# Routing of the first half at the end of a scan, last logits among the first expert tiles, and two projections of kept chunks per step, in a two-layer graph and expert kernel

## The chip, the cores and the metric

The kernel runs on one core of one Trainium2 chip. The metric is device time in microseconds (us) of one execution. The core has a matrix engine (PE, with its weight loads shown as PEld), a vector engine (DVE), an activation engine (ACT), a general engine (POOL), and a queue that issues transfers (SP). They run side by side and wait for one another by semaphores; each works through its own queue in order.

## The reference

Input are x, 4096 tokens of 256 features, and an adjacency matrix of 4096 x 4096. Two layers follow one another; each is a graph part and an expert part, both added to x:

```python
x = x + L0_gnn(layernorm(x), adj)      # relu(adj @ x @ gcn_w + b), layernorm, mamba
x = x + L0_ffn(layernorm(x))           # top 2 of 8 experts, D=256, H=512, gelu
x = x + L1_gnn(layernorm(x), adj)      # filtered adjacency, projections, relu
x = x + L1_ffn(layernorm(x))           # top 2 of 6 experts, three layers
```

The mamba of layer 0 is a recurrence over the tokens with 512 channels and 16 states each:

```python
def step(hst, inp):
    dAt, dBut, Ct = inp
    hst = dAt * hst + dBut
    return (hst, hst @ Ct)
...
y = ys + u * D_skip
y = y * jax.nn.silu(z)
return y @ w_out
```

The expert part of layer 0 takes softmax of `xf @ gate_w + gate_b`, keeps each token's two largest, and adds `weight * (gelu(xf @ w1 + b1) @ w2 + b2)` of both experts.

## The kernel before

**The scan.** The 4096 tokens are cut into eight chunks c = 0 to 7 of 512. A chunk has 32 steps i = 0 to 31; a step is one channel block m (four blocks of 128) and a pair of states. Per step ACT makes two tiles da (L1154), DVE runs the recurrence twice (L1161) and multiplies by C (hc, L1171), POOL makes db (L1138), and PE adds the products up in PSUM (L1188, `Step.total`). At the end of a block DVE multiplies by silu(z) (`Step.gate`, L1197). The region is written as a manual schedule: each engine executes in the order in which the loop over n = 32c + i issues.

**Tails.** The output projection of chunks 0 to 5 is put off: their gated outputs are kept in device memory (`keep_gated`). From chunk 6's step 8 on, `Tail.step` works through a list of tails, one entry per scan step: two entries with a product on PE (L929, and the residual by an identity matmul, L933), one `put` (ACT copies PSUM with a sum, L938; stores x1d, L943), and at the next step `squares` (L948, L952). The first three chunks have one idle entry more. Chunk 6's own tails are put into the list at chunk 7's step 5, behind the kept ones. `Norm` normalizes rows of chunks 0 to 6 during chunk 7 (L985), transposes them (L998) and makes router logits (L1010); `Last` does the projection of chunk 7, its first half at steps 22 and 25 and its second half (`add`, L1063) behind the scan's last gates. `Last.norm` makes the statistics of chunk 7 (L1077 to L1082), its normed rows (L1087), their store (L1091), the transposes (L1097), logits (L1104), and x1d's last rows (L1110, L1112).

**Routing of the first half.** `Dispatch.choose` (by `router`, L110 to L138) finds the two experts of tokens; `place` counts them by two matmuls (L231, L235) and a chain of twelve DVE operations (L240 to L266); `one_hot` writes four groups of one-hot rows (L273); `tables` (a generator, L311 to L424) makes the list of tiles by expert, compares slots (L359, L363, L364), multiplies with the one-hots on PE (L369), and from that makes `src`, the row numbers to gather (L381 to L387), the bias sums (L395, L400) and `dst`. They follow the scan in program order: choose, place, `last.norm`, one_hot, tables; the engines' queues then hold them in an order set by a scheduler.

**Expert tiles.** `expert_tiles` goes through tiles of 256 rows of one expert: gather by `src` (L430, POOL), weights and bias (L532, L535, SP), transposes (L539), a copy to xkT (L543), first product ps_h (L518) with gelu (L522), second product ps_y (L503) of the tile before, bias (L508), store (L439). The first nine tiles are of the first half's tokens (part0[0]), the others of all tokens. Between tiles `then0` takes pieces of `others()`: choose, place, one_hot for the second and third batch, and their tables. Layer 1's adjacency tiles (L1498, L1504, L1505, L1506) are worked on beside them, and layer 1's propagation (L1516) comes after.

Of the kernel before, what the change touches and what calls it, by code (L numbers as in the profile page):

```python
# [9 lines left out]
F32 = mybir.dt.float32  # L10
# [20 lines left out]
def kernel(ctx: ExitStack, tc: tile.TileContext, out: bass.AP, **a):  # L31
# [73 lines left out]
    def router(ps, bias_b, E, rev, renorm, oh, wv, pool):  # L105
# [4 lines left out]
        nc.vector.tensor_tensor(lg, ps, bias_b.unsqueeze(1).to_broadcast([P, T, E]), ALU.add)  # L110
# [8 lines left out]
        nc.scalar.activation(lg, lg, AF.Exp)  # L119
        nc.vector.tensor_reduce(col(1), lg, AX.X, ALU.add)  # L120
# [6 lines left out]
        for i in range(2):  # L127
# [6 lines left out]
            if i == 0:  # L134
                nc.vector.scalar_tensor_tensor(lg, hots[0], -4.0, p, ALU.mult, ALU.add)
                q = lg
        if not renorm:
# [25 lines left out]
    class Dispatch:  # L163
# [47 lines left out]
        def choose(self, b, logits, bias_b, renorm, pool):  # L211
            T, t0 = self.T[b], self.t0[b]
            hots = self.oh[b][:, 1:, :].rearrange("p (t i) e -> p t i e", i=2)
            router(
                logits, bias_b, self.E, self.rev[:, :T, :], renorm, hots,
                self.wv[:, t0:t0 + T, :], pool,
            )

        def place(self, b, psum, tag, pool):

# [6 lines left out]
            if (2 * G + 1) * E <= CW:  # L227
                tot = ps[:, G * E:]
            else:
                tot = psum.tile([P, CW], F32, name="ps_pl1", tag=tag)  # L230
# [6 lines left out]
            )  # L237
            flat = pool.tile([P, E * (G + 1)], F32, name=f"pl_at{G}")
# [15 lines left out]
            )  # L254
            row = pool.tile([P, G], F32, name=f"pl_row{G}")
# [13 lines left out]
        def one_hot(self, b):  # L269

            g0, G, S, row = 2 * self.t0[b], 2 * self.T[b], 2 * TPC, self.row.pop(b)
            for g in range(0, G, S):
# [3 lines left out]
                )  # L276

    class Part:
# [14 lines left out]
        def tables(self, ps, tp, biases, NG, other=None, hots=None):  # L293
# [4 lines left out]
            if hots is None:  # L298
                def hots(shape):
                    return tp.tile(list(shape), BF16, name="tb_eq", bufs=3)  # L300
# [27 lines left out]
            nc.vector.tensor_reduce(ex, ge[:, :, 1:], AX.X, ALU.add)  # L328
            oh = ge[:, :, :E]
# [23 lines left out]
            S = 2 * TPC  # L353
            group = dp.group.rearrange("p t i -> p (t i)")
            slots = slot.rearrange("p f h -> p (f h)").unsqueeze(1).to_broadcast([P, S, C])
            for g0 in range(0, NG, S):
# [11 lines left out]
                for g in range(S):  # L368
                    nc.tensor.matmul(  # L369
                        ps[:, :2 * C], dp.lo[:, g0 + g, :], eq[:, :2, g, :],  # L370
                        start=(g0 + g == 0), stop=(g0 + g == NG - 1),
                    )
# [15 lines left out]
            nc.vector.tensor_scalar(ex, ex, float(E - 1), None, ALU.min)  # L388
            nc.vector.tensor_copy(self.exps, ex)
# [104 lines left out]
    def expert_tiles(jobs, psum, pool, weights, bias_out, layers, kb_out, also=None):  # L494
# [16 lines left out]
        def layer(w, xT, mb, func, bias, name):  # L511
            hT = pool.tile([P, mb, TR], F32, name=name)
            for mm in range(mb // 2):
                ps = ps_h.tile([P, 2, TR], F32, name="ps_h")
                for j in range(2):
                    m = 2 * mm + j
                    for d in range(DB):
                        nc.tensor.matmul(  # L518
                            ps[:, j, :], w[:, d, m * P:(m + 1) * P], xT[:, d, :],
                            start=(d == 0), stop=(d == DB - 1),  # L520
                        )
# [1273 lines left out]
```

## Time and profile before

| what | value |
| --- | --- |
| three runs, device time | 2415.34, 2420.55 (median), 2423.94 us |
| profiled execution, device time | 2412.49 us |
| its span | 2410.7 us |
| PE busy in the span | 2239.3 us (93%) |
| DVE busy | 1648.1 us (68%) |
| ACT busy | 1194.8 us (50%) |
| POOL busy | 1144.8 us (47%) |
| scan's recurrence, L1161 | 512 instructions, 1266 ns each |
| hc, L1171 | 256 instructions, 1281 ns each |
| first product of the tiles, L518 | 864 matmuls, 388 ns each |
| gelu's line L522, first wait | 11.39 us idle before it, at 1288.88 us |

The span runs from the first to the last instruction of the profiled execution; the 1.8 us between it and the device time lie around it. A duration is that of one instruction, and matmuls overlap, so their durations are longer than the distance between two of them: a group of x8 that shows 1.89 us in sum is the length of the group. In lines of the timeline, the bracket tells how long the engine was idle before the group and which instruction released it. The windows give busy time of each engine between two times.

### The profile page before, as it was taken

What the parts mean: (1) busy time and instruction counts of PE and PEld (TensorE: products, weight loads), DVE (VectorE), ACT (ScalarE), POOL (GpSimd) and SP (SyncE); (2) the same over time, 40 slices, a digit from 0 to 9 for tenths busy, and PEclk for the clock granted to TensorE, in tenths of its full rate; (3) what the DMA queues carried; (4) which work ended last, traced back from release to release, by engine and by line L of the source; (5) the groups of instructions that cost most, each with busy time, mean ns of one, the idle gap of its engine ahead of it and who ended that gap; (6) DMA issues with size and microseconds to landing.
All of it is one profiled execution on the core that took longest, in us unless ns stands there. A gap on an engine that the chain in (4) does not pass through costs nothing. (4 is left out here: it accounts for less than half of the span.)

```text
span 2410.7 us, 28097 instructions
## 1 busy us (share of the span) xinstructions
PE 2239.3 (93%) x9018; PEld 1624.2 (67%) x9018; DVE 1648.1 (68%) x2455; ACT 1194.8 (50%) x2050; POOL 1144.8 (47%) x828
## 2 busy tenths in 40 slices
PE   8999999999999999896997999799999999999985
PEld 7665665656465665553666888667888888877774
DVE  2069999999999999998986411291666667742233
ACT  4255666574655666574753322145555555532321
POOL 1057777777877787775644555310000000045652
PEclk9999999999999999998997999999999999999998
DMA  7279999999999999996848877551444444456786
GB/s 237 83 228 227 241 275 238 274 243 268 247 260 258 238 274 238 271 269 174 270 136 266 295 231 228 162 166 53 143 146 148 146 145 146 148 170 209 230 274 235
DMA packets 293071, 511.58 MB, mean 212 GB/s; under 512 B 25376, under 2 KB 159648, under 8 KB 292016
## 3 DMA queue, kind: packets, MB, share of 16 engines
q1 hardware_dynamic: 246640, 412.64, 54.5%
q0 software_dynamic: 46272, 97.03, 18.7%
q8 instruction: 75, 1.23, 0.2%
q14 instruction: 84, 0.69, 0.1%
HBM read 406.03 MB, written 44.83 MB: 187 GB/s over the span
## 5 line engine op out<-in xcount | busy, mean ns | idle before, releaser
L1138 POOL TENSOR_TENSOR db<-du,bb 128x1024 f32<-128x1024 f32 x256 | 607.1, 2372 | 329.5 <-DVE hc L1171 83.1
L1161 DVE TENSOR_TENSOR_SCAN db<-da,state,db 128x512 f32<-128x512 f32 x512 | 627.2, 1266 | 31.5 <-ACT da L1154 29.3
L671 PE MATMUL pt<-at,gn 128*128 128x256 f32 x2048 | 479.4, 387 | 14.9 <-ACT gn L87 9.2
L671 PEld LDWEIGHTS pt<-at,gn 128*128 128x128 f32 x2048 | 397.1, 195 | 135.7 <-issue 63.1
L1154 ACT ACTIVATE da<-dt,negA 128x512 f32<-128x512 f32 x512 | 346.4, 688 | 249.5 <-DVE db L1161 238.7
L1516 PE MATMUL pf<-gn,f 128*128 128x256 f32 x2048 | 452.0, 380 | 0.0
L1516 PEld LDWEIGHTS pf<-gn,f 128*128 128x128 f32 x2048 | 386.6, 190 | 57.2 <-issue 6.4
L1171 DVE TENSOR_TENSOR hc<-db,cb 128x1024 f32<-128x1024 f32 x256 | 328.0, 1281 | 18.2 <-issue 0.4
L1188 PE MATMUL psy<-hc,ident 128*128 128x512 f32 x576 | 301.6, 618 | 4.6 <-DMA hc<-hc 3.7
L81 POOL TENSOR_TENSOR ln_rs<-ln_rs,mhalf 128x4 f32<-128x4 f32 (+1 forms) x25 | 33.4, 1335 | 507.6 <-DVE ln_rs L80 507.1
L508 DVE TENSOR_TENSOR yk<-ps_y,bk 128x512 f32<-128x512 f32 x73 | 50.4, 691 | 308.9 <-PE ps_y L503 232.2
L1505 ACT ACTIVATE f<-f 128x1024 f32<-128x1024 f32 x128 | 134.6, 1057 | 198.7 <-DVE f L1504 128.2
L518 PE MATMUL ps_h<-xkT,wk 128*128 128x256 f32 x864 | 213.6, 388 | 14.7 <-DVE xkT L543 6.9
L503 PE MATMUL ps_y<-wk,hk 128*128 128x256 f32 x864 | 213.3, 382 | 9.2 <-ACT hk L522 6.6
L1175 POOL DMA_DIRECT2D hc<-hc x224 | 195.0, 870 | 0.2
L518 PEld LDWEIGHTS ps_h<-xkT,wk 128*128 128x128 f32 x864 | 159.1, 192 | 50.6 <-ACT hk L522 11.3
L1504 DVE TENSOR_SCALAR f<-at 128x1024 f32<-128x1024 f32 x128 | 88.1, 688 | 148.0 <-PE pf L1516 134.4
L503 PEld LDWEIGHTS ps_y<-wk,hk 128*128 128x128 f32 x864 | 161.9, 191 | 32.7 <-ACT hk L522 8.4
L1188 PEld LDWEIGHTS psy<-hc,ident 128*128 128x128 f32 x576 | 109.3, 196 | 90.2 <-issue 64.0
L1511 DVE SCALAR_TENSOR_TENSOR cnt<-at,cnt 128x1024 bf16<-128x1024 f32 x120 | 145.9, 1216 | 15.9 <-DMA at<-in_adjT_dram 12.3
L1506 ACT ACTIVATE f<-f 128x1024 f32<-128x1024 f32 x128 | 134.5, 1055 | 3.4
L787 PE MATMUL ps_xz<-hT,w_in 128*128 128x512 f32 x256 | 116.3, 597 | 15.2 <-ACT hT L771 8.8
(321 smaller groups left out, 2513.6 us busy)
## 6 DMA issues: line engine op xcount, KB each, us to landing
at<-in_adjT_dram SPq DMA_DIRECT2D x256, 512.0 KB
bb<-bcd SPq DMA_DIRECT2D x128, 512.0 KB
cb<-bcd SPq DMA_DIRECT2D x128, 512.0 KB
hc<-hc POOLq DMA_DIRECT2D x224, 256.0 KB
wk<-in_L_ffn_W_dram SPq DMA_DIRECT2D x70, 512.0 KB
wk<-in_L_ffn_expert_w_dram SPq DMA_DIRECT2D x114, 256.0 KB
yg<-d_ys SPq DMA_DIRECT2D x14, 512.0 KB
yd<-us SPq DMA_DIRECT2D x6, 1024.0 KB
```

The costliest lines, as they stand in the source:

```text
L503: nc.tensor.matmul(ps[:, j, :], hT[:, m, j * P:(j + 1) * P], w[:, m, :], start=(m == 0), stop=(m == kb_out - 1),)
L518: nc.tensor.matmul(ps[:, j, :], w[:, d, m * P:(m + 1) * P], xT[:, d, :], start=(d == 0), stop=(d == DB - 1),)
L671: nc.tensor.matmul(pt[:, k, :], xl[:, j, k * P:(k + 1) * P], at[:, jj, :], start=(j == 0 and k == 0), stop=(j == NT - 1 and k == DB - 1),)
L1138: nc.gpsimd.tensor_tensor(self.db, self.f.du[self.half][:, self.mi:self.mi + 1, :].to_broadcast([P, 2, CW]), self.bb, ALU.mult,)
L1154: nc.scalar.activation(da, self.f.dt[self.half][:, self.mi, :], AF.Exp, scale=negA[:, self.m, n:n + 1])
L1161: nc.vector.tensor_tensor_scan(self.db[:, j, :], da, self.db[:, j, :], state[:, self.m, n:n + 1], ALU.mult, ALU.add,)
L1171: nc.vector.tensor_tensor(self.hc, self.db, self.cb, ALU.mult)
L1175: nc.gpsimd.dma_start(self.hc[:, 0, :], self.hc[:, 1, :], accum_op=ALU.add)
L1188: nc.tensor.matmul(f.psy[m], ident, self.hc[:, j, :], start=False, stop=(self.g == GS - 1 and j == last),)
L1505: nc.scalar.activation(f, f, AF.Square)
L1511: nc.vector.scalar_tensor_tensor(cnt, at, 0.0, cnt, ALU.is_gt, ALU.add)
L1516: nc.tensor.matmul(pf[:, t, :], f[:, jj, t * P:(t + 1) * P], gn[:, j, :], start=(j == 0 and t % 2 == 0), stop=(j == NT - 1 and t % 2 == 1),)
```

## The change

Five things are changed together.

1. `router`, `place` and `one_hot` become generators (`choosing`, `placing`, `one_hots`), and a new generator `first_half` strings them together with the tables. The scan's loop takes one step of it at chunk 7's steps 24, 26, 28 and 31 (the router in three parts, then the place's two matmuls), takes two more before the last gates (the place's DVE chain), and the others after the gates and after the last projection.
2. `tables` gets `held`: the products with the one-hots (`products`) are issued together when all comparisons are done, into a PSUM bank that is asked for only then. The number of experts of tiles (`exps`) is written earlier. Its scratch tiles, and the first two gathered tiles `ready`, lie in the unused half of `gn` (`Carve`), and the two gathers are issued before `last.norm`.
3. `Last.norm` loses transposes and logits. Its normed rows are loaded back from device memory, and `logits7` makes the logits between the second and third batch's routing. Its stores go out on ACT's queue in place of SP's.
4. The router of the second batch, the bias sums' consumer and the second tiles' transposes are given an explicit order (`behind`, `turned`, `begun`); `then0` takes four pieces per tile from the second tile on, where it took three from the first. The order of PSUM pools changes, and the bank tag of `Last.first` (d2 to d0).
5. `TAILS`: two steps of `Tail.step` per scan step from chunk 6's step 24 to 31, none at chunk 7's steps 0 to 3.

```diff
-    def router(ps, bias_b, E, rev, renorm, oh, wv, pool):
+    def router(ps, bias_b, E, rev, renorm, oh, wv, pool, behind=None):
...
-        nc.vector.tensor_tensor(lg, ps, bias_b.unsqueeze(1).to_broadcast([P, T, E]), ALU.add)
+        op = nc.vector.tensor_tensor(lg, ps, bias_b.unsqueeze(1).to_broadcast([P, T, E]), ALU.add)
+        if behind is not None:
+            after(op, behind)
...
         nc.scalar.activation(lg, lg, AF.Exp)
+        yield
...
+        def placing(self, b, psum, tag, pool, second=None):
...
+                psum, tag = second or (psum, tag)
                 tot = psum.tile([P, CW], F32, name="ps_pl1", tag=tag)
...
+            yield
             flat = pool.tile([P, E * (G + 1)], F32, name=f"pl_at{G}")
...
-        def tables(self, ps, tp, biases, NG, other=None, hots=None):
+        def tables(self, ps, tp, biases, NG, other=None, hots=None, held=False):
...
+            nc.vector.tensor_scalar(ex, ex, float(E - 1), None, ALU.min)
+            nc.vector.tensor_copy(self.exps, ex)
...
+                eqs[g0] = eq
+                if not held:
+                    products(ps, g0)
+                yield
+            if held:
+                ps = ps()
+                for g0 in range(0, NG, S):
+                    products(ps, g0)
                 yield
...
-            nc.vector.tensor_scalar(ex, ex, float(E - 1), None, ALU.min)
-            nc.vector.tensor_copy(self.exps, ex)
...
-            xk = pool.tile([P, 2, D], F32, name="xk", bufs=4)
-            dp.fetch(k, xk)
+            if ready:
+                xk = ready.pop(0)
+            else:
+                xk = pool.tile([P, 2, D], F32, name="xk", bufs=4)
+                dp.fetch(k, xk)
...
+                    if d == 0 and j == 0 and given and 2 <= len(turned) < 4:
+                        after(op, begun[len(turned) - 2])
...
+        TAILS = {(NC - 2, i): 2 for i in range(24, STEPS)}
+        TAILS.update({(NC - 1, i): 0 for i in range(4)})
...
-                    nc.sync.dma_start(tokens(dp.xd, c)[:, t0:t0 + 2, :], xn[:, :2, :])
-                    ps_t = (ps_m if hh == 0 else ps_a).tile(
-                        [P, DB, HW], F32, name="ps_xnT7", tag=("m0", "d0")[hh]
-                    )
...
+                    nc.scalar.dma_start(tokens(dp.xd, c)[:, t0:t0 + 2, :], xn[:, :2, :])
...
-                    nc.sync.dma_start(rows, self.xr[hh])
+                    nc.scalar.dma_start(rows, self.xr[hh])
+
+        def first_half(biases):
+
+            yield from dp.choosing(0, lgs[:, :dp.T[0], :], gate_b, False, ra)
+            yield
+            yield from dp.placing(0, ps_m, "m0", ra, (ps_m, "m1"))
+            yield
+            table = part0[0].tables(
+                lambda: ps_m.tile([P, CW], F32, name="ps_inv", tag="m0"),
+                room, biases, NT, held=True,
+            )
+            next(table)
+            for _ in dp.one_hots(0):
+                next(table)
+            yield
+            yield from table
...
-                Tail.step(tails)
+
+                for _ in range(TAILS.get((c, i), 1)):
+                    Tail.step(tails)
...
+                    if i in (24, 26, 28, STEPS - 1):
+                        next(firsts)
...
+            next(firsts)
+            next(firsts)
             for k in gated:
                 steps[k].gate()
+            next(firsts)
             for m in range(H, MB):
                 for hh in range(2):
                     last.add(hh, m)
-        dp.lo = onehots
-        dp.choose(0, lgs[:, :dp.T[0], :], gate_b, False, ra)
-        dp.place(0, ps_y, "psy", ra)
+            next(firsts)
+            next(firsts)
+            ready = [room.tile([P, 2, D], F32, name="xk", bufs=2) for _ in range(2)]
+            for k, xk in enumerate(ready):
+                part0[0].fetch(k, xk)
         last.norm()
...
+            def logits7(xn):
+                xT = rp.tile([P, 2, DB, HW], F32, name="xnT7", bufs=1)
+                for hh in range(2):
+                    ps = inverse().rearrange("p (k t) -> p k t", k=DB)
...
+                    nc.scalar.copy(xT[:, hh], ps)
+                    yield
...
+                nc.scalar.copy(lgs[:, NT - TPC:, :], ps)
+                yield
+
             def others():
 
+
+                xn = rp.tile([P, TPC, D], F32, name="xn7", bufs=1)
+                nc.sync.dma_start(xn, tokens(dp.xd, NC - 1))
                 for b in (1, 2):
+                    if b == 2:
+                        yield from logits7(xn)
                     t0 = dp.t0[b]
-                    dp.choose(b, lgs[:, t0:t0 + dp.T[b], :], gate_b, False, rp)
+                    dp.choose(b, lgs[:, t0:t0 + dp.T[b], :], gate_b, False, rp, turned[0])
...
-                if n < FIRST0 - 2:
-                    for _ in range(3):
+                if 0 < n < FIRST0 - 2:
+                    for _ in range(4):
                         next(pieces, None)
```

## The prediction

> **What bounds the kernel now.** Four views, in this order: the page's busy shares, the windows by stage, the timeline between the scan and the first tiles, and the timeline of a stall in the scan's last chunk.
>
> PE is busy 93% of the span, DVE 68%: PE is the bound on average, so what counts is where PE does not work. The windows say where. The columns are length, then busy time of PE, PEld, DVE, ACT, POOL, the granted clock, DMA share and GB/s:
>
> ```profile
> 1060.00:1080.00 20.00, 20.00 (x60) 10.15 (x59) 16.04 (x13) 16.86 (x35) 13.48 (x10) 1.00 1.02 286
> 1080.00:1100.00 20.00, 11.13 (x31) 6.32 (x29) 19.55 (x17) 14.44 (x28) 9.71 (x7) 0.84 0.86 221
> 1100.00:1120.00 20.00, 8.81 (x26) 5.80 (x26) 19.73 (x18) 9.40 (x27) 17.25 (x8) 0.76 0.65 171
> 1140.00:1160.00 20.00, 20.00 (x64) 11.79 (x63) 14.50 (x12) 16.18 (x38) 9.41 (x4) 1.00 0.60 193
> 1256.00:1286.70 30.70, 11.18 (x67) 7.46 (x66) 21.94 (x117) 9.88 (x19) 9.77 (x10) 0.58 0.60 196
> 1345.00:1500.00 155.00, 153.48 (x750) 132.00 (x749) 37.41 (x52) 43.98 (x88) 83.19 (x84) 1.00 0.80 251
> ```
>
> In the scan the bound is DVE (19.55 of 20), except at 1140 to 1160, where it has only 14.50 of work: it waits there. From 1080 to 1120 PE has 20 us of room. From 1256 to 1286.7 PE works 11.18 of 30.70 us at a clock of 0.58: this is the gap between the scan's end and the first expert tile. From there on the tiles are bound by PE (153.48 of 155).
>
> The gap, link by link (start, duration, engine, line, operation; idle before it in brackets):
>
> ```profile
> 1245.63 1.23 DVE L1171 TENSOR_TENSOR hc<-db,cb 128x1024 f32<-128x1024 f32 x1
> 1247.13 5.40 PE L1188 MATMUL psy<-hc,ident 128*128 128x512 f32 x12
> 1252.36 3.62 PE L1063 MATMUL ps_out<-w_out,us 128*128 128x256 f32 x16
> 1256.93 0.70 DVE L240 TENSOR_TENSOR_SCAN pl_at<-onesf,ps_pl 128x264 f32<-128x264 f32 x1 [0.48 <-PE ps_pl L235]
> 1262.36 4.62 DVE L273 TENSOR_TENSOR gn<-iota,pl_row 128x1024 bf16<-128x1024 f32 x4
> 1275.21 0.17 DVE L387 CAST d0f_src<-tb_tok 128x18 int32<-128x18 f32 x1
> 1276.34 1.18 POOL L430 DMA_INDIRECT xk<-d_xdf,d0f_src  x1 [15.75 <-DVE d_oh L133]
> 1283.01 0.48 PE L539 MATMUL ps_xt<-ident,xk 128*128 128x128 f32 x1 [5.98 <-DMA xk<-d_xdf,d0f_src]
> 1285.28 0.69 DVE L543 COPY xkT<-ps_xt 128x512 f32<-128x512 f32 x1 [5.78 <-issue]
> 1286.92 5.02 PE L518 MATMUL ps_h<-xkT,wk 128*128 128x256 f32 x12
> 1288.88 0.47 ACT L522 ACTIVATE hk<-ps_h,d0f_b 128x256 f32<-128x256 f32 x1 [11.39 <-issue]
> ```
>
> The last hc (scan's end), totals, last projection, then the place chain, one-hots, tables, src, the gather (6.67 us from issue to the transpose), xkT, first ps_h. DVE is the chain's carrier from 1256.9 to 1275.4.
>
> The stall in chunk 7:
>
> ```profile
> 1137.28 1.89 PE L929 MATMUL ps_out<-w_out,at 128*128 128x256 f32 x8
> 1139.64 0.39 ACT L938 ACTIVATE xr<-ps_out 128x256 f32<-128x256 f32 x1 [5.45 <-PE ps_out L933]
> 1141.16 2.46 DVE L1161 TENSOR_TENSOR_SCAN db<-da,state,db 128x512 f32<-128x512 f32 x2 [7.83 <-ACT da L1154]
> 1148.07 1.28 ACT L811 ACT_TABLE_LOAD   x1
> ```
>
> A kept product (1.89 us and 0.59 for the residual, 2.48) stands late on PE; ACT's put waits for it, da stands behind the put, and the scan waits 7.83 us for da.
>
> [...]ps_h x8 takes 3.62 us from 1286.92 and 1.89 in full tiles; but the clock also halved around 1232, behind 1.19 us of full idleness among thin matmuls. [...]here the load is 1.28 and the next activation starts 1.30 after it, so I take 1.28. [...]the table operations agree, 0.15 to 0.22 us whether 8 or 72 elements. [...]the gather here takes 6.67, and that is used.
>
> **The change, part by part.** The sum is made on the profiled execution: 2412.5 us (span 2410.7), 8.1 below the median 2420.55 of the three runs.
>
> 1. Places at the scan's end. The router's twenty operations of the first half already stand among the last scan steps (the last at 1245.45), so they move little. The place's two matmuls (0.61 + 0.64, now at 1255.8) go ahead of the last two totals: PE would do one total (1.8), the two matmuls, then the other totals, so they end at about 1250.2 (1248.4 if ahead of all three). The place's twelve DVE operations add up to 3.87 us (0.70, 0.15, 0.41, 0.14, 0.41, 0.61, 0.59 and five of 0.17); they run from 1250.2 to 1254.1. Both gates (0.69 each, now 1250.84 and 1252.56) are queued behind them on DVE: 1254.1 and 1254.8. The last projection waits for the gates and ends about 2.5 us later than 1256.0; from 1.25 (PE alone) to 3.6 (if PE's clock halves while it waits). Behind it stand the norm of chunk 7 and its stores.
>
> 2. Tables behind the gates. From 1254.8: tables some 20 operations at 0.16 = 3.3, chunk 7's statistics between them 2.0, one-hots 4.62 and the pairs at L359/L364 8 x 0.3 = 2.4 with 1.3 for ACT's L363 between: 8.3. That is 1268.4; products 0.4, the seven operations to src 1.6 (1273.68 to 1275.38 now, whose way held an f at L1504): src at about 1270.4, against 1275.38. **5.0 us earlier**; 4.4 to 7 by the bounds of part 1 and of the interleaving.
>
> 3. From src to PE at work. The gather follows 5.0 earlier, xkT is there at about 1280.9, and ps_h could start at 1282. But the bias sums, the router of the second batch and f are moved behind xkT, and ACT has Exp (0.27), L1505 and L1506 (1.06 each) and a table load (1.28) ahead of the first gelu. From 1280.9: three router operations to 1281.6, f (0.69) by 1283.0, the two of ACT to 1285.1, the load to 1286.4. The first gelu is then 2.5 us earlier than 1288.88, not 5.0. PE has five groups to do until it needs it, so part of the rest survives: I take **-3.0**, bounds -5.0 and 0. The lower end of the gain is the weights: on SP's queue the reload of chunk 7's normed rows, which waits for the last stores, is put ahead of at, b1 and wk (now 1270.85), so wk goes out at 1272 to 1274, and when wk landed is not shown.
>
> 4. Last logits among the tiles. Eight transposes (1.04 in the trace for such eight) and sixteen matmuls (1.85) leave a stage where PE idles and enter one where PE is the bound: **+2.9**. An Exp of the second batch among gelus needs two table loads, 2.56 us on ACT, which is busy 43.98 of 155 there; ps_h's three buffers hide most: **+0.4** (0 to 1.5).
>
> 5. Tails. Two steps per scan step from chunk 6's i24, none in chunk 7's i0 to i3; the kept ones end at i19 of chunk 7, not i23. In chunk 7 the put no longer stands ahead of da at 1139.6: ACT goes from zs (1134.2) over the squares (1.6) to da, and the scan resumes near 1136 instead of 1141.2. The next put still waits for a product behind the second zs group (PE at about 1147.7), with a table load behind it, so scan steps that now start at 1153.4 and 1157.4 start at about 1150.5 and 1154.2: **-3.2** (-5 to 0). PE freed at i20 to i23 (4 x 2.48) lies beside a scan bound by DVE: **-0.6** (0 to -1.2, DVE's idle time at 1200 to 1220). In chunk 6 the added products find PE full until 1080 and put and squares (2.8 us per tail) find ACT at 16.86 of 20; after 1081 there is room: **+0.5** (0 to 9.9, four steps of 2.48 if all is handed to the scan).
>
> Sum: -3.0 + 2.9 + 0.4 - 3.2 - 0.6 + 0.5 = -3.0. On the profiled execution 2409.5, on the scale of the median **2417.5**.
>
> **Rivals.** No change means within 0.3%, 7.3 us, about what these runs tell apart (they spread over 8.6).
>
> - *Faster, 2410.5.* The 5.0 us of src come through whole because PE's five groups and a warmer clock cover gelu's wait, part of the logits' matmuls (2) fill holes in the first tile, and the stall at 1141 goes nearly whole: -5.0 + 0.9 + 0.4 - 5.0 - 1.2 = about -10. For it: PE's clock of 0.58 in the gap. Against: ACT's queue ahead of the first gelu.
> - *Slower, 2430.* The same stall in a new place: chunk 6, i24 to i31. Every second tail step is a put that waits on ACT for products on a full PE, with da behind it; four doubled steps are 9.9 us of backlog until PE has room, and DVE, busy 19.55 of 20 from 1080 on, can't make that up. With chunk 7's gain used up by the same lateness: -3.0 + 3.3 - 0.6 + 9.9 = +9.6. It decides from 7.6 us lost there. For it: PE 20.00 of 20 and ACT 16.86 in 1060 to 1080. Against: DVE has 4 us idle there already, and PE's room begins at 1081.
> - *It doesn't reach its aim, 2424.* src is earlier, but wk lands late or gelu waits in full, and the tails give nothing: 0 + 2.9 + 0.4 = +3.3.
>
> **Numbers.** Forecast 0.40 (own range 2411 to 2424), faster rival 0.28, slower 0.24, the last 0.08. Faster: 0.05 of the forecast and 0.25 of the first rival, 0.30. Slower: 0.22 of its rival and 0.02 each of forecast and the last, 0.26. Within: 0.44. The range, 2405 to 2431, reaches beyond the centres of both rivals and leaves out about 0.07 below and 0.12 above.
>
> **What would show it.** src's cast near 1270 after a scan's end at the old distance; the last projection's end 2.5 us later against the last hc; a first gelu with an idle time that ends with f's L1506 and the load; tiles with 2.9 us of transposes and thin matmuls among them; in chunk 7 a longest wait of the scan under 4 us. I am wrong if chunk 6's scan waits for da by more than 7 us, if ps_h waits for wk, or if gates start after 1255.5.

## The result and the profile after

| what | before | after |
| --- | --- | --- |
| median of 10 runs each, same chip | 2418.26 us | 2429.73 us |
| lowest and highest | 2410.71, 2423.94 us | 2425.27, 2434.25 us |
| profiled execution, its span | 2412.49, 2410.7 us | 2431.11, 2429.3 us |

The ratio of the times is 1.0048, with a 95% interval of 1.0034 to 1.0062: the change costs about 11.5 us. The profiled execution of after lies near its median, that of before 6 us below its own, so the two profiles differ by 18.6 us, more than the kernels do. What can be followed step by step is the stretch up to the tenth expert tile. There after is 11.05 us late, and that figure holds unchanged from tile 10 (1372 us in before) to tile 35 (1553 us). Another 3.3 us appear up to the second layer's first tile and about 4 in its tiles; these I don't explain, and they are of the size by which single runs differ.

First the page's first part, busy time by engine. PE has the same 9018 matmuls as before and 9.1 us more busy time in an 18.6 us longer span. So one half of the difference is PE standing still, and the other is the same matmuls taking longer:

```profile
PE 2248.4 (93%) x9018; PEld 1629.5 (67%) x9018; DVE 1658.1 (68%) x2455; ACT 1197.5 (49%) x2051; POOL 1143.8 (47%) x828
```

Then marks on both timelines. "hc i23" is the start of hc at step 23 of chunk 7, before the first router operation of the changed kernel; hc i31 is the scan's end; "yk" is the copy of a tile's second product.

| mark | before | after | after later by |
| --- | --- | --- | --- |
| hc, chunk 6 i31 | 1103.29 | 1106.84 | +3.55 |
| hc, chunk 7 i23 | 1211.87 | 1209.34 | -2.53 |
| hc, chunk 7 i31 | 1245.63 | 1250.41 | +4.78 |
| end of the last projection | 1256.0 | 1262.2 | +6.2 |
| end of src's cast | 1275.38 | 1272.28 | -3.1 |
| first ps_h | 1286.92 | 1283.71 | -3.2 |
| first gelu | 1288.88 | 1289.93 | +1.05 |
| first yk | 1299.97 | 1301.66 | +1.69 |
| yk of tile 10 | 1372.41 | 1383.46 | +11.05 |

Two stretches lose: i23 to i31 (+7.3) and the tiles (+9.4). The tables gain 9.3 between the last projection and src; 4.9 of it is given back between ps_h and the first yk.

**The last scan steps.** The timeline of after on DVE and POOL (start, duration, engine, line, operation, idle before it):

```profile
1214.38 2.35 POOL L1207 TENSOR_TENSOR db<-du,bb 128x1024 f32<-128x1024 f32 x1 [1.32 <-ACT xnT L1076]
1214.81 2.07 DVE L121 TENSOR_TENSOR rt_lg<-rt_lg,rt_red 128x128 f32<-128x128 f32 x1
...
1223.71 1.21 DVE L1240 TENSOR_TENSOR hc<-db,cb 128x1024 f32<-128x1024 f32 x1
1225.06 2.34 POOL L1207 TENSOR_TENSOR db<-du,bb 128x1024 f32<-128x1024 f32 x1 [1.29 <-issue]
1225.15 0.26 DVE L125 RECIPROCAL rt_red<-rt_red 128x16 f32<-128x16 f32 x1
1225.45 2.10 DVE L127 TENSOR_TENSOR rt_p<-rt_lg,rt_red 128x128 f32<-128x128 f32 x1
1227.58 0.29 DVE L133 TENSOR_REDUCE rt_red<-rt_p 128x16 f32<-128x128 f32 x1
1227.90 0.29 DVE L134 TENSOR_TENSOR d_oh<-rt_p,rt_red 128x128 bf16<-128x128 f32 x1
...
1229.41 2.45 DVE L1230 TENSOR_TENSOR_SCAN db<-da,state,db 128x512 f32<-128x512 f32 x2
...
1237.01 2.35 POOL L1207 TENSOR_TENSOR db<-du,bb 128x1024 f32<-128x1024 f32 x1 [1.32 <-ACT state L1236]
1237.11 2.39 DVE L134 TENSOR_TENSOR d_oh<-rt_lg,rt_red 128x128 bf16<-128x128 f32 x1
```

Between the hc at 1223.71 and the next scan at 1229.41 nine router operations stand in one block. The router has eighteen operations on DVE. Three of them, one per block, take 2.07, 2.10 and 2.39 us instead of the 0.29 that the same kind takes at 1227.90. Each is a tensor_tensor with both operands in SBUF, starts 0.10 to 0.43 us after POOL's db, and ends some 0.15 us after it: 1225.45 + 2.10 = 1227.55, POOL at 1227.40. These three db start 0.12 to 0.14 us after the end of an hc: hc releases them, though the brackets name other instructions. The reciprocal beside the same POOL instruction takes 0.26. In before the same operations stand one to four at a time, nine of them behind an hc and nine between the scan and hc (timelines of before, DVE and POOL):

```profile
1211.87 1.23 DVE L1171 TENSOR_TENSOR hc<-db,cb 128x1024 f32<-128x1024 f32 x1
1213.65 0.29 DVE L118 TENSOR_TENSOR rt_lg<-rt_lg,rt_red 128x128 f32<-128x128 f32 x1
1215.27 2.35 POOL L1138 TENSOR_TENSOR db<-du,bb 128x1024 f32<-128x1024 f32 x1 [3.39 <-ACT state L1167]
...
1230.48 0.27 DVE L130 TENSOR_TENSOR d_oh<-rt_lg,rt_red 128x128 bf16<-128x128 f32 x1
1230.66 1.23 DVE L1171 TENSOR_TENSOR hc<-db,cb 128x1024 f32<-128x1024 f32 x1
1231.81 2.45 DVE L1161 TENSOR_TENSOR_SCAN db<-da,state,db 128x512 f32<-128x512 f32 x2
1234.18 0.36 DVE L131 TENSOR_TENSOR d_oh<-d_oh,d_rev 128x128 bf16<-128x128 bf16 x1
1234.46 1.21 DVE L1171 TENSOR_TENSOR hc<-db,cb 128x1024 f32<-128x1024 f32 x1
```

The operation at 1213.65 stands third behind an hc, as the one at 1214.81 of after does. It isn't stretched, because POOL's db comes only at 1215.27 here. So the place behind hc does harm only if db has started by then. Of before's nine, only two reductions start behind it (1223.63 and 1227.91), and they keep their 0.29. A single operation between scan and hc costs next to nothing: hc starts 2.55 us (1228.11 to 1230.66) or 2.65 us (1231.81 to 1234.46) after its scan, against 2.54 without one (1233.11 to 1235.65 in after). A step without router work takes 3.69 us (1235.65 - 1231.96 in after), eight of them 29.5: from hc i23 to hc i31 before takes 33.8, after 41.1. Of before's 33.8, 1.0 isn't the router's: a wait of 0.61 for da at i24, and an hc there of 1.59 us.

**The scan's waits.** The view of waits on DVE, for chunk 6's end (from 1055 us on) and then for chunk 7 (from 1095), first in before and then in after; columns are the waiting instruction, what it waited for, us in total, how often, and the longest:

```profile
DVE db L1161 <- ACT da L1154: 4.0, 2, 2.4
DVE db L1161 <- ACT da L1154: 12.7, 5, 7.8
...
DVE db L1230 <- ACT da L1223: 7.2, 3, 2.7
DVE db L1230 <- ACT da L1223: 6.6, 3, 3.6
```

The longest wait of chunk 7 has gone from 7.8 to 3.6 us and the sum of its waits from 12.7 to 6.6; half of that gain was lost again in chunk 6, where the sum rose from 4.0 to 7.2.

**The gap.** The timeline of after from the last hc to the first gelu:

```profile
1250.41 1.23 DVE L1240 TENSOR_TENSOR hc<-db,cb 128x1024 f32<-128x1024 f32 x1
1253.72 0.70 DVE L255 TENSOR_TENSOR_SCAN pl_at<-onesf,ps_pl 128x264 f32<-128x264 f32 x1 [2.09 <-PE ps_pl L249]
1257.70 1.28 DVE L1266 TENSOR_TENSOR us<-psy,zs 128x512 f32<-128x512 f32 x2
1258.44 3.72 PE L1135 MATMUL ps_out<-w_out,us 128*128 128x256 f32 x16 [0.60 <-DVE us L1266]
1272.10 0.18 DVE L447 CAST d0f_src<-gn 128x18 int32<-128x18 f32 x1
1277.43 0.48 PE L604 MATMUL ps_xt<-ident,gn 128*128 128x128 f32 x1 [6.66 <-DMA gn<-d_xdf,d0f_src]
1283.71 3.62 PE L578 MATMUL ps_h<-xkT,wk 128*128 128x256 f32 x8
1286.47 1.06 ACT L1615 ACTIVATE f<-f 128x1024 f32<-128x1024 f32 x1 [0.89 <-issue]
1287.56 1.06 ACT L1616 ACTIVATE f<-f 128x1024 f32<-128x1024 f32 x1
1288.63 1.28 ACT L584 ACT_TABLE_LOAD   x1
1289.93 0.84 ACT L584 ACTIVATE hk<-ps_h,d0f_b 128x256 f32<-128x256 f32 x2
1290.45 7.72 PE L578 MATMUL ps_h<-xkT,wk 128*128 128x256 f32 x22 [1.08 <-ACT hk L584]
```

The places' chain stands ahead of the gates, src is there 21.9 us after the last hc (29.8 before), and ACT then has two f and a table load ahead of the first gelu: PE begins 3.2 us earlier than before. Then it stands for 0.85 us until a bias sum is there and for 1.08 us until the first gelu is.

**The first tiles.** The windows of after: gap, ps_h to the first yk, and from there to tile 10's yk. The columns are length, then busy time of PE, PEld, DVE, ACT and POOL, the granted clock, DMA share and GB/s; the last two lines are the same two tile stretches of before:

```profile
1262.10:1283.70 21.60, 3.94 (x41) 3.02 (x41) 11.63 (x48) 4.54 (x10) 10.13 (x11) 0.57 0.56 178
1283.70:1301.66 17.96, 16.03 (x51) 12.10 (x50) 6.22 (x29) 7.33 (x12) 3.23 (x4) 0.66 0.86 284
1301.66:1383.46 81.80, 75.92 (x418) 63.22 (x417) 53.35 (x140) 31.01 (x56) 39.65 (x36) 1.00 0.84 278
...
1286.90:1299.97 13.07, 13.07 (x53) 10.89 (x52) 5.90 (x22) 3.79 (x8) 3.89 (x4) 0.82 0.45 152
1299.97:1372.41 72.44, 70.92 (x390) 60.40 (x389) 45.06 (x108) 27.02 (x50) 39.07 (x36) 1.00 0.94 318
```

The second stretch takes 4.9 us longer in after: PE stands for 1.9 us, and is busy 3.0 us longer with about as many matmuls (51 against 53), at a clock of 0.66 against 0.82. The third has 5.0 us more matmuls and 4.4 more idle time. What that is, from the timeline of after:

```profile
1309.74 0.60 PE L1466 MATMUL ps_inv<-ident,xn 128*128 128x128 f32 x4
1311.05 1.92 PE L1476 MATMUL ps_inv<-gate_w,xnT 128*128 128x8 f32 x16
1332.17 0.69 DVE L1614 TENSOR_SCALAR f<-at 128x1024 f32<-128x1024 f32 x1 [2.33 <-DMA at<-in_adjT_dram]
1332.90 1.06 ACT L1615 ACTIVATE f<-f 128x1024 f32<-128x1024 f32 x1 [5.95 <-DVE f L1614]
1334.37 1.99 PE L578 MATMUL ps_h<-xkT,wk 128*128 128x256 f32 x8 [2.38 <-ACT hk L584]
```

The last logits stand there with two groups of transposes and sixteen thin matmuls, 2.7 us of PE by the distance of starts (0.44 + 0.44 + 1.78). The second batch's place, which before has in the gap (1276.40), is there too (two matmuls from 1301.46, 0.46 us). At 1334.37 PE waited 2.38 us for a gelu that stood on ACT behind an f, whose own input had waited for a transfer.

### The profile page after: what moved, and what is told of

Read it like the earlier page. It is cut to its first block, busy times and chain, and to the rows that moved or that the text cites. A ratio compares the mean times of both kernels' runs of the same rounds, so it can differ in the third digit from the quotient of the medians.

```text
span 2429.3 us, 28087 instructions
## 1 busy us (share of the span) xinstructions
PE 2248.4 (93%) x9018; PEld 1629.5 (67%) x9018; DVE 1658.1 (68%) x2455; ACT 1197.5 (49%) x2051; POOL 1143.8 (47%) x828
## 3 DMA queue, kind: packets, MB, share of 16 engines
q10 hardware_dynamic: 1088, 1.05, 0.1%
## 5 line engine op out<-in xcount | busy, mean ns | idle before, releaser
L1240 DVE TENSOR_TENSOR hc<-db,cb 128x1024 f32<-128x1024 f32 x256 | 327.1, 1278 | 18.4 <-issue 0.3
L578 PE MATMUL ps_h<-xkT,wk 128*128 128x256 f32 x864 | 219.1, 396 | 22.1 <-DVE xkT L611 10.7
L563 PEld LDWEIGHTS ps_y<-wk,hk 128*128 128x128 f32 x864 | 162.3, 192 | 31.8 <-issue 6.1
L1616 ACT ACTIVATE f<-f 128x1024 f32<-128x1024 f32 x128 | 134.5, 1055 | 3.5
```

Source lines behind the costliest of these rows:

```text
L563: nc.tensor.matmul(ps[:, j, :], hT[:, m, j * P:(j + 1) * P], w[:, m, :], start=(m == 0), stop=(m == kb_out - 1),)
L578: op = nc.tensor.matmul(ps[:, j, :], w[:, d, m * P:(m + 1) * P], xT[:, d, :], start=(d == 0), stop=(d == DB - 1),)
L1240: nc.vector.tensor_tensor(self.hc, self.db, self.cb, ALU.mult)
```

## The experiments

Each kernel was timed beside the kernel before on the same chip, so the ratios can be set side by side, but absolute times of different chips can't. Differences in us are those of the medians; the ratio isn't the quotient of the medians, and the two can differ by a microsecond or so. After's own figure is +11.5 us (ratio 1.0034 to 1.0062). Code is cut where three dots stand.

**1 and 2. The tails alone.** Without the doubled steps in after, and with nothing but them in before:

```diff
-        TAILS = {(NC - 2, i): 2 for i in range(24, STEPS)}
-        TAILS.update({(NC - 1, i): 0 for i in range(4)})
+        TAILS = {}
```

> The changed kernel with one tail step in every scan step again (as before the change); all else as changed. Theory: the doubled tails cost 3.6 us in chunk 6 and gave back 7.6 us by chunk 7's step 24 (4.1 us net), so without them the last hc starts about 4 us later than in the changed kernel (at about 1254) and the time is about 4 us longer, some 15 us above the kernel before. Rival: the doubled tails are the loss (3.6 us in chunk 6, nothing kept at the end), and the time falls to about 8 us above the kernel before.

```diff
+        TAILS = {(NC - 2, i): 2 for i in range(24, STEPS)}
+        TAILS.update({(NC - 1, i): 0 for i in range(4)})
...
-                Tail.step(tails)
+                for _ in range(TAILS.get((c, i), 1)):
+                    Tail.step(tails)
```

> The kernel before with the doubled tails alone. Theory: the stall of 7.83 us in chunk 7 shrinks more than chunk 6 loses; last hc near 1242, time about 4 us below the kernel before. Rival: chunk 7's other waits take it back before the scan's end, and the time is within 1 us of the kernel before, or above it by chunk 6's 3.6 us.

After without them: 2417.07 us against 2400.34, ratio 1.0073 (1.0058 to 1.0089), +16.7. Before with them: 2395.95, ratio 0.9981 (0.9973 to 0.9988), -4.4. From both sides the tails are worth 4 to 5 us, a gain, though after's interval and that of experiment 1 overlap; the tails are not why after is slower. The other parts cost about 16 together.

The gain of experiment 2 isn't all from shorter waits. From 980 us to the scan's end its waits for da sum to 15.4 us, against 17.4 in before, but its last hc comes 6.4 us earlier (1239.27), or 5.1 counted from the last hc of chunk 5. The rest lies in the last steps: in before the scheduler places the router, and with other tails it places it otherwise. Here mostly one operation stands ahead of each hc, and eight of the eighteen stand behind the last hc, and from hc i23 (1209.07) to i31 it takes 30.2 us. So against before with the same tails, after's last steps lose 10.9 us and not only 7.3.

**3. The router spread over the steps.** After, with a yield behind every router operation, and three of them ahead of each hc from i24 to i29 in place of three blocks behind it:

```diff
         nc.vector.reciprocal(col(1), col(1))
+        yield
...
+                if c == NC - 1 and 24 <= i < 30:
+                    for _ in range(3):
+                        next(firsts)
                 cur.product()
...
-                    if i in (24, 26, 28, STEPS - 1):
+                    if i == STEPS - 1:
                         next(firsts)
```

> The changed kernel, its router of the first half issued three operations per scan step (chunk 7, i24 to i29), each trio between the scans and hc, in place of three blocks behind hc at i24, i26 and i28. Theory: the blocks cost the scan 7.6 us from i26 to i29, most of it by their place; spread they cost about 2 to 3 us, last hc near 1244.5, time about 6 us below the changed kernel, some 5 us above the kernel before. Rival: 18 operations of about 0.3 us cost their 5.4 us wherever they stand on DVE; the time falls by no more than 2 us.

2406.33 against 2400.34, ratio 1.0023 (1.0014 to 1.0032), +6.0: about half of after's loss is gone, and the intervals don't meet (1.0034 is after's lower end). DVE's timeline of this kernel at two of the three operations:

```profile
1217.28 0.26 DVE L128 RECIPROCAL rt_red<-rt_red 128x16 f32<-128x16 f32 x1
1217.57 0.29 DVE L131 TENSOR_TENSOR rt_p<-rt_lg,rt_red 128x128 f32<-128x128 f32 x1
...
1230.43 0.29 DVE L140 TENSOR_TENSOR d_oh<-rt_lg,rt_red 128x128 bf16<-128x128 f32 x1
```

From hc i23 (1208.67) to hc i31 (1242.43) it takes 33.8 us, as long as before takes, but more than the 30.2 of experiment 2, where the operations stand singly.

**4. The same blocks, but ahead of hc.** To tell the length of the blocks from the stretched operations:

```diff
+                if c == NC - 1 and i in (24, 26, 28):
+                    next(firsts)
                 cur.product()
...
-                    if i in (24, 26, 28, STEPS - 1):
+                    if i == STEPS - 1:
```

> The changed kernel with the same three router blocks in the same scan steps, but issued ahead of hc in place of behind it. Behind hc two of their operations took 2.10 and 2.39 us, and ended with POOL's db, which hc releases. Theory[...]: ahead of hc no db of POOL runs beside them, both take about 0.3 us, and the last hc comes 3.5 to 4 us earlier (near 1246.6), the time about 4 us below the changed kernel. Rival: they are long for another reason (their operands, a semaphore), the durations stay above 2 us and the time does not move by more than 1 us.

2407.10, ratio 1.0030 (1.0022 to 1.0039), +6.8. The same two operations, on DVE's timeline of this kernel:

```profile
1219.47 0.29 DVE L127 TENSOR_TENSOR rt_p<-rt_lg,rt_red 128x128 f32<-128x128 f32 x1
1229.13 0.29 DVE L134 TENSOR_TENSOR d_oh<-rt_lg,rt_red 128x128 bf16<-128x128 f32 x1
```

The blocks are as long as in after, but the three operations start behind the end of POOL's db (at 1210.61, 1219.47 and 1229.13, where db ends at 1210.10, 1218.93 and 1229.05) and take 0.29 us each, and hc i23 to i31 takes 35.1 us (1206.38 to 1241.47). So of the 7.3 us lost in after, 6.0 come from the blocks' place behind hc; the three stretched operations are 2.07 + 2.10 + 2.39 - 3 x 0.29 = 5.7 of them. The other 1.3 us are a balance: before has its 1.0 of other waits in this stretch, and here an x_shift of only 128x4 falls beside POOL's db and takes 0.93 us (1218.02; 0.93 in after too, at 1222.86, and 0.14 in before, at 1226.20). So the blocks' length is worth some 1.5. The interval of this ratio overlaps after's, so it is this stretch of the trace that carries the reading, not the time alone.

**5, 6 and 7. What loses in the tiles.** All three stand on experiment 3. In 5 the first two f's squares go behind given gelus on ACT; in 6 transposes and logits go back into the gap, and the reload of the normed rows is gone; 7 has both.

```diff
+    gelus = []
...
-                nc.scalar.activation(f, f, AF.Square)
+                sq = nc.scalar.activation(f, f, AF.Square)
+                if c == 0 and j2 < 2:
+                    after(sq, gelus[(3, 31)[j2]])
```

> The kernel of e3 with one order more: on ACT the first adjacency tile's squares (f, Square and Tanh) come behind the first tile's four gelus, and the second's behind the eighth tile's last gelu. Theory: f and its table load held the first gelu by some 2 us, and a second f, waiting for its transfer, held a gelu in the fifth tile (PE idle 2.38 us); both go, the time falls by 3 to 4 us against e3, to about 2 us above the kernel before. Rival: other work (bias sums, the Exp of the second batch) holds the gelu as long, and the tables of the second part hold the tiles: the time moves by less than 1 us.

```diff
+                    for k in range(DB):
+                        for j in range(2):
+                            nc.tensor.transpose(
+                                ps_t[:, k, j * P:(j + 1) * P], xn[:, j, k * P:(k + 1) * P], ident
+                            )
+                    xT = w1p.tile([P, DB, HW], F32, name="xnT7", tag=("h", "hT")[hh])
+                    nc.scalar.copy(xT, ps_t)
...
-                xn = rp.tile([P, TPC, D], F32, name="xn7", bufs=1)
-                nc.sync.dma_start(xn, tokens(dp.xd, NC - 1))
...
-                    if b == 2:
-                        yield from logits7(xn)
```

> The kernel of e3 with the last chunk's transposes and logits back between the last projection and the first tile, as in the kernel before; no reload, the second and third batch routed without it. Theory: 2.6 us of PE's work leave the tiles, the reload leaves SP's queue ahead of the weights, and the two table loads of a late Exp go (2.56 us on ACT with gelus behind it): tiles gain 3 to 6 us, src comes up to 1 us later, time 3 to 5 us below e3. Rival: the thin matmuls fitted in PE's holes, and in the gap they delay src: the time is within 1 us of e3.

> Both of e5 and e6 on the kernel of e3. Theory: the two are different waits and add up: 6 to 9 us below e3, so 0 to 3 us below the kernel before. Rival: one wait stands behind the other, and both together give no more than the better one alone.

| kernel | median, before beside it 2400.28 | ratio (95%) |
| --- | --- | --- |
| 5, first f later | 2401.99 | 1.0009 (1.0000 to 1.0017) |
| 6, logits in the gap | 2398.42 | 0.9987 (0.9978 to 0.9996) |
| 7, both | 2397.31 | 0.9987 (0.9981 to 0.9994) |

Against experiment 3's +6.0, 5 gains 4.3 (the two intervals overlap a little) and 6 gains 7.9. From the first yk to tile 10's, experiment 3 loses 10.6 us against before and experiment 6 loses 3.9. So moving the logits costs 6.7 us in the tiles, of which their own matmuls are 2.7. By the medians both changes together give 1.1 us more than 6 alone, and by the ratios nothing more. That looks as if one wait stood behind the other, but the traces don't show it. In 5 the first yk comes 3.1 us earlier after the last hc than in 3, and from there to tile 10 it takes 2.3 us longer. In 7 against 6 the first yk is 1.3 us later and that stretch 2.4 shorter. So up to tile 10 the late f gains about 1 us with the logits among the tiles (0.7) and without them (1.1). Where the rest of 5's 4.3 us lies isn't known. PE's waits in 6 (from 1278 to 1365 us) show what is left:

```profile
PE ps_h L588 <- DVE xkT L621: 2.9, 1, 2.9
PE ps_h L588 <- ACT hk L594: 2.5, 1, 2.5
PE ps_h L588 <- DVE d0f_b L468: 1.4, 1, 1.4
```

Two of the three stand in the first tiles, before the first yk. Which operation on which queue makes the 4.0 us that the logits cost beyond their matmuls isn't separated; their copies on ACT, the reload's place on SP and the router behind them all went with the edit.

**8. Doubled steps later, pauses at the stall.** Before, with doubled steps only at chunk 6's i28 to i31, and none at chunk 7's i5 to i8 (the loop changed as in experiment 2):

```diff
+        TAILS = {(NC - 2, i): 2 for i in range(28, STEPS)}
+        TAILS.update({(NC - 1, i): 0 for i in range(5, 9)})
```

> The kernel before with doubled tail steps only at chunk 6's i28 to i31 and none at chunk 7's i5 to i8, where the stall was. Theory: chunk 6 no longer pays 3.6 us (PE has room from 1081 on) and chunk 7's products don't stand in front of da's: time 6 to 8 us below the kernel before, 2 to 4 below e2. Rival: without tails the silu's table loads and the zs copies hold the scan at the same place, and the time is that of e2 or above.

2401.17 against 2400.28, ratio 1.0008 (1.0000 to 1.0017). No gain. hc at chunk 7's i6 is 6.7 us late, 4.6 ahead at i9, and only 1.7 ahead at the end. It loses 2.9 us at i20, where the scan waits 2.80 us for POOL's db (idle until a transfer had brought bb), and 2.4 at i27, where a router operation fell beside POOL's db of 1223.71 to 1226.06 (DVE's timeline of 8):

```profile
1223.81 2.40 DVE L133 TENSOR_TENSOR d_oh<-d_rev,rt_red 128x128 bf16<-128x128 f32 x1
```

So the stretched operation appears in a kernel with before's code for the router too, once other tails make the scheduler put it behind an hc with db running. A stall moved is not a stall removed.

**9 and 10. Smaller cuts ahead of the first gelu.** 9 is experiment 7 with the experts' bias loaded before the scan ends; 10 also lets the router of the second batches go without waiting for the first turned tile (xkT).

```diff
-            b1s = []
+            b1 = load(small, a["L0_ffn_b1"], "b1")
+            b1s = [b1]
...
-            b1 = load(wp, a["L0_ffn_b1"], "b1")
-            b1s.append(b1)
```

> The kernel of e7 with the experts' first bias loaded before the scan, so that the bias sums of the first tiles (L463, L468) can run on DVE while the gather is under way, in place of behind xkT. Theory: in e7 the first gelu (1282.98) waits for the bias sum and the table load behind it, and PE stands 0.94 us for the second sum; with early sums the first gelu comes about 1 us earlier and the time falls by 0.5 to 2 us against e7, to 3.5 to 5 us below the kernel before. Rival: the Exp of the second batch holds the table load just as long; no change above 0.5 us.

```diff
-                    dp.choose(b, lgs[:, t0:t0 + dp.T[b], :], gate_b, False, rp, turned[0])
+                    dp.choose(b, lgs[:, t0:t0 + dp.T[b], :], gate_b, False, rp)
```

> The kernel of e9 with the second and third batch's router no longer held behind the first xkT: its Exp, and with it gelu's table load, can run while the gather is under way. Theory: the first gelu then waits for PE alone, comes 2 to 3 us earlier than in e7, and the time falls by 1 to 3 us against e9. Rival: the router's operations get in the way of src on DVE and the gather starts later by as much; time as e9 or above.

9: 2413.57 against 2414.30, ratio 0.9996 (0.9984 to 1.0007); 10: 2410.17, ratio 0.9988 (0.9977 to 0.9999). Neither can be told from experiment 7's 0.9987. In 9's trace the first gelu does come 1.7 us earlier after the last hc than in 7 (37.85 against 39.54). But PE then stands 1.64 us for a transfer of weights and 3.98 us for a gelu behind an f, and the first yk comes 2.0 us later (54.21 against 52.18). So the bias did hold the first gelu, and freeing it gained nothing while those waits stood behind it.

**11 and 12. One step of the tails.** Experiments 11 and 12 ask whether the stall of before comes from which entry of the tails falls on which scan step. Experiment 11 is before with a single added tail step (the loop changed as in experiment 2), at chunk 6's i28, so that the entries in chunk 7 come one scan step earlier; 12 is experiment 10 with this in place of the eight doubled steps:

```diff
+        TAILS = {(NC - 2, 28): 2}
```

> The kernel before with one tail step more at chunk 6's i28 and none left out. Tails go in cycles of product, product, put; e2's eight extra steps less four left out shift the cycle at chunk 7's i4 by one, as one extra step does. Theory: the stall in chunk 7 depends on whether a put stands behind its product between the two groups of zs copies, so one step of shift removes the 7.83 us wait as in e2, without e2's 3.6 us loss in chunk 6: last hc 6 to 8 us earlier than in the kernel before, time 5 to 8 us below it. Rival: the four steps less between i0 and i3 matter too (PE is late there without them), and the time is between the kernel before and e2.

> The kernel of e10 with the same single extra tail step in place of the eight doubled and four empty ones. Theory: as e11, the scan's gain grows by chunk 6's 3.6 us, time some 3 us below e10. Rival: e10's other parts are hidden behind the gather and the tiles, and it ends above e11.

11: 2409.27 against 2416.48, ratio 0.9969 (0.9955 to 0.9983), -7.2. 12: 2411.77, ratio 0.9979 (0.9969 to 0.9989), -4.7. The size in 11 is what was expected, the way isn't. DVE's timeline of 11 in chunk 7:

```profile
1137.14 2.46 DVE L1162 TENSOR_TENSOR_SCAN db<-da,state,db 128x512 f32<-128x512 f32 x2 [7.40 <-ACT da L1155]
...
1151.47 2.46 DVE L1162 TENSOR_TENSOR_SCAN db<-da,state,db 128x512 f32<-128x512 f32 x2 [2.81 <-ACT da L1155]
```

The long wait is still there, one step earlier (7.40 in place of 7.83), and one wait of 2.81 us follows it where before has two, of 2.15 and 1.79. From 980 us on the scan's waits sum to 15.0 us in five, against 17.4 in eight, and the last hc is 4.8 us earlier. Of these, 1.9 us are there from i9 to i18. Of the others, 2.0 come between hc i23 and i31 (31.8 us against 33.8): a wait of 0.61 is gone there, and the scheduler again places the router otherwise, with seven of its operations behind the last hc. The first gate is 6.4 us earlier (1244.40 against 1250.84), since PE is done with a group of thin logits sooner and starts the last totals at 1240.69, by the last hc and not 1.5 us behind it. The remaining 0.8 us I can't place. So what one tail step gains here is in part the luck of where the scheduler then puts other work. Experiment 11 has the lowest ratio of all and is faster than both kernels, though its interval overlaps those of 12 and of 2.

## Why the prediction was wrong

The forecast was 3.0 us faster; it is 11.5 slower. Its sum, put against the marks of the two timelines:

| term | predicted | measured |
| --- | --- | --- |
| tails, to hc i23 (-3.2 - 0.6 + 0.5) | -3.3 | -2.5 |
| router of the first half, hc i23 to i31 | 0 | +7.3 |
| scan's end to PE at work (parts 1 to 3) | -3.0 | -3.1 |
| tiles (2.9 + 0.4) | +3.3 | +9.4 |
| sum | -3.0 | +11.1 |

**The step that failed is the first sentence of part 1**: "The router's twenty operations of the first half already stand among the last scan steps (the last at 1245.45), so they move little". They (eighteen on DVE) stand there in both kernels, but before has them in small groups of which POOL's db stretches none, and after in three blocks behind hc, which releases db. That costs 7.3 us; experiment 3 spreads them again and has the 33.8 us of before, and experiment 4 shows that 6.0 belong to the place behind an hc whose db has started. I had read in the diff at which steps the blocks are issued, and priced a move by its distance in steps, not by what runs on the other engines at that moment. What passes between the two engines there isn't shown by the traces; they show the durations: 2.10 us for a tensor_tensor of 128x128 where POOL's db was first (1225.45 in after), 0.29 for the same one where it wasn't (1219.47 in experiment 4), and 0.26 for a reciprocal, with one input, beside the same db (1225.15 in after). Before's trace showed it already: L974's x_shift, a tensor_tensor of 128x4, takes 0.14 us at 1226.20 and 0.92 at 1199.24, beside POOL's db of 1197.80 to 1200.15. The step missed was to look at such a spread of one form and ask what ran beside it.

**A term of part 4 was mis-sized**: "+2.9" and "+0.4" for the logits among the tiles measured 9.4 with all that moved there. The matmuls' own price was about right (2.7). The error is the rest: I took PE's three ps_h buffers for cover of all that ACT and DVE get to do there. PE's idle time in the stretch went from 1.5 to 5.9 us, 2.38 of it in one wait for a gelu behind an f; of the longer matmul time, the second batch's place is at most 0.5 us, and 1.8 I can't itemise. Experiment 6, set against 3, shows 6.7 us of the loss to be the moved logits' with what goes along with them: copies, reload and table loads.

**The gap came out right in sum**, with -3.1 against -3.0, but by errors that cancel. The last projection came 1.4 us later against the last hc, not 2.5; src came 7.9 us earlier against the scan's end, not 5.0; and ps_h to the first yk grew by 4.9, where 2.0 was allowed. Waits are 1.9 of it. The other 3.0 is the same matmuls taking longer at a lower clock, which part 3 left out: busy time times clock is alike in both, 16.03 x 0.66 = 10.6 and 13.07 x 0.82 = 10.7. That ACT's f and the table load would stand ahead of the gelu was the right late link, at the right lines.

**The tails were right in direction and nearly in size**: -2.5 on these timelines, -4.4 and -5.2 by experiments 2 and 1. That the size is near is luck in part: chunk 6 cost 3.6 us where +0.5 stood, and chunk 7 up to i23 gained 6.1 where 3.8 stood. The longest wait in chunk 7 is 3.6 us, under the 4 that was named. The waits at chunk 6's end reach 7.2 us in sum, but before has 4.0 there, and none is longer than 2.7. The slower rival's mechanism, a stall moved to chunk 6, is there too, but with 3.6 us where it needed 7.6 to decide: the kernel is slower by about as much as that rival said, for another reason. The sign named as one that would show me wrong, gates later than 1255.5, did appear (1257.70), but from the scan's late end: against the last hc the gates are 7.3 us late, less than the 8.5 forecast.

## What to carry to other kernels

A handful of small operations that fill holes singly can be nearly free (here 0.01 to 0.11 us for one between scan and hc), and the same handful in a block costs its length (in experiment 4 eighteen of about 0.29 us, in a stretch of 35.1 us that takes 29.5 without router work), with the rest of a POOL instruction on top if that has started beside it (three of them took 5.7 us more in after): ask of a moved operation what runs on the other engines where it lands. Work moved out of an idle gap into a stage bound by one engine can cost more than its time on that engine (here 6.7 us for 2.7 us of matmuls). Which of the things that go with it (copies, table loads, a transfer) made the other 4.0 us isn't separated here, so ask of each what it stands ahead of in its engine's queue. Before restructuring around a stall between a scan and a background task, shift the task by one step: here one added step gave 7 us where the whole change lost 11. Then look at what else the shift moved, for here a part of the 7 came from the router's operations.

## What the runs showed of the hardware that was not expected

A DVE tensor_tensor of 128x128 took 0.29 us with no POOL instruction beside it (1227.90 in after) and 2.07 to 2.39 beside a POOL tensor_tensor that started first: seven to eight times its price, set by what was left of POOL's 2.35 us (all three ended 0.14 to 0.15 us after it) and not by its own size (x_shift, of 128x4, took 0.92 us at 1199.24 in before and ended 0.01 us after POOL's db). It repeats from run to run (2.09, 2.10 and 2.40 in experiment 1, 2.40 in 8). Reductions and a reciprocal in the same place kept their 0.26 to 0.29 us (1216.93 and 1227.91 in before, 1225.15 in after). So did the recurrence, which reads one operand from PSUM: 2.45 us for two at 1196.88 in before, beside POOL's db of 1197.80 to 1200.15, and 2.45 at 1229.41 in after with no db beside it. But not every operation with one input was safe: the tensor_scalar x_dev of 128x4 took 0.45 us at 1216.60 in experiment 3, beside a db that ended at 1217.03, and 0.14 at 1219.17 in after, with no POOL instruction beside it.
